# Where the third and fourth chunk of the attention output are split, and which buffers the last stretch splits into: a two-layer graph attention kernel

## The chip, the core and the metric

The kernel runs on one core of a Trainium2 chip. The metric is the device time of one execution in microseconds (us). TensorE (PE) does the matrix products and has a row of its own, PEld, for its weight loads. VectorE (DVE), ScalarE (ACT) and GpSimd (POOL) do the element work, and the queue of SyncE (SP) issues most of the remaining transfers.

## The reference

The input `x` is 64 matrices of 256 x 512 in fp32, `adj` is one 256 x 256 matrix of zeros and ones, and all five weights are 512 x 512.

```
# layer 0
q, k, v = x @ Wq + bq, x @ Wk + bk, x @ Wv + bv          # 8 heads of 64
scores  = q k^T / sqrt(64) + (1 - adj) * -1e9
o       = softmax(scores) v                                # per head, then side by side
x       = layernorm(x + o @ Wo + bo)
# layer 1
y       = adj @ x
x       = layernorm(x + y @ weight + bias)
```

## The kernel before

**Pairs and windows.** The 64 matrices are handled as 32 pairs (`NP` = 32), so that a product has 512 rows. The work is software-pipelined in windows: window `w` holds the attention of pair `w`, the v, q and k products of pair `w+1` ("ahead"), and the products with `Wo` (name "o") and with layer 1's weight (name "l") of pair `w-1` ("behind"). Windows 1 to 30 have one pattern, written out as a list of steps in `between` (L540); `last_window` (L598) finishes pairs 30 and 31, with a list of its own. The 29 windows from 2 to 30 have the same first half.

**Three parts.** An fp32 product is made of three passes in a faster matmul type. A left operand is split into three tiles by four instructions: on VectorE `cut` (the upper bits, L168), `low` (the rest, L169) and `diff` (L174), and on ScalarE `high`, a copy of `cut` (L298 or L278). The weights lie split in DRAM and are streamed in, three tiles of 1 MB for each product.

**Blocks.** One product of one of four row or column groups is a block (L532). `near` (L317) is eight matmuls, four with the low part and four with the high part, and then a ScalarE instruction that scales the PSUM bank (L326). `far` (L328) is the four matmuls with the diff part, and the evacuation: for "o" and "l" a VectorE addition onto the residual `r` (L338), in the last two pairs L342. `far` lags behind: `block` appends to `LAGGED`, and `caught_up(n)` (L524) works the list down to n entries. In a list of steps `f1` is `caught_up(1)` and `f0` or `f` is `caught_up(0)`. Four PSUM banks (`ps_mm`) serve all blocks, so the bank of a block must have been evacuated before the fourth block after it starts.

**Chunks.** `chunk_parts` (L284) splits one chunk of the attention output (`co[j]` or "o" chunk j below) or of adj @ x (`cl[j]`). Its tiles come from pools of their own: three buffers for high and low (`chunks`), four for diff (`differences`), and a single buffer for `cut`. The parts of x (`x_parts`, `x_diff`) come from another pool, `parts`, with four buffers each. What of x's four chunks does not fit in its window is kept in `PENDING` for the next one: from window 2 on its list is one chunk, `x_t` (a transpose, L264), `x_parts` and `x_diff`.

**Slots.** A slot is one quarter of a pair's attention: `values` of the unit before (sums with ones at L394, values at L402), then `scores` of its own (L367), exponentials on ScalarE (L371). `masked` (L374) multiplies each of the two tiles of exponentials with the mask on VectorE, `summed` (L380) adds the two. The next slot's first matmuls (L394) need that sum `sm`.

**Due times.** Such follow-up work is put off by `later(n, f)`, and falls due at the n-th `tick` after it. A tick follows every block, slot and `adj_x` step (L592), but not a `chunk_parts`, an x step or a `caught_up`. The first tick after a slot is its own, so `later(1, ...)` in a slot runs directly behind it.

**Whose order is written.** In windows 1 to 30 the orders of TensorE, ScalarE and VectorE are those of the list (`manual_schedule`, L639). In the last window only TensorE's order is written; the compiler's scheduler orders the others by readiness and by their place in the list.

Of the kernel before, what the change touches and what calls it, by code (L numbers as in the profile page):

```python
# [21 lines left out]
F32R = mybir.dt.float32r  # L22
# [5 lines left out]
P = 128  # L28
# [15 lines left out]
def fast(tc, x, adj, wq, bq, wk, bk, wv, bv, wo, bo, w1, b1, out):  # L44

    nc = tc.nc
    B, N, D = x.shape
# [3 lines left out]
    NP = B // 2  # L51
# [15 lines left out]
    parts = pool("parts", 4)  # L67
    chunks = pool("chunks", 3)
    differences = pool("differences", 4)
# [96 lines left out]
    def cut_low(a, cut, low):  # L166

        nc.vector.tensor_scalar(cut.bitcast(I32), a.bitcast(I32), -int(FINE), None, op0=OP.bitwise_and)  # L168
        nc.vector.tensor_tensor(low, a, cut, op=OP.subtract)  # L169

    def difference(a, low, diff):


        nc.vector.scalar_tensor_tensor(diff, low.bitcast(F32), -(FINE + 1), a, op0=OP.mult, op1=OP.add)  # L174
# [50 lines left out]
    def later(n, f, *args):  # L225
        due.append([n, f, args])
# [9 lines left out]
    BANKS = {}  # L236

    def x_t(p, i):  # L240
        xs = XC.pop((p, i))
        if p == 0:
            pt = ps_mm.tile([P, DC, P], F32, name="mm")
            if i == 0:
                for d in range(DC):
                    if d % 2 == 0:
                        t = qk.tile([P, 2, D], F32, name="kT")
                    XF[p, d] = t[:, d % 2]
            for d in range(DC):
                nc.tensor.transpose(pt[:, d, :], xs[:, d * P:(d + 1) * P], ident)  # L250
            for d in range(DC):
                to = XF[p, d][:, i * P:(i + 1) * P]
                if d % 2:
                    nc.scalar.activation(to, pt[:, d], AF.Copy)
                else:
                    nc.vector.tensor_copy(to, pt[:, d])
        else:
            if p > 1:
                XF[p, i] = xpool.tile([P, D], F32, name="xT")
                XC[p, i] = xs  # L260
            elif i % 2 == 0:
                t = four.tile([P, 2, D], F32, name="o")
                XF[p, i], XF[p, i + 1] = t[:, 0], t[:, 1]
            nc.vector.transpose(XF[p, i], xs)  # L264
            if p == 1:
                load_next()
# [17 lines left out]
    def chunk_parts(name, p, j):  # L284

        a = (O if name == "o" else Y)[p, j // 2][:, j % 2].rearrange("p k i -> p (k i)")
        cut = one.tile([P, D], F32, name="cut")
        high, low = (chunks.tile([P, D], F32R, name=n) for n in ("chigh", "clow"))
        diff = differences.tile([P, D], F32R, name="cdiff")
        cut_low(a, cut, low)  # L290
        difference(a, low, diff)
        CP[name, p, j] = high, low, diff
        CUT[name, p, j] = cut
        later(1, chunk_high, name, p, j)
# [64 lines left out]
    def scores(p, u):  # L359
        g, b = UNITS[u]  # L360
        for kc in range(NC):

            sc = [ps_at.tile([P, 2, N], F32, name="at") for s in range(2)]
            for a in range(2):
                for s in range(2):
                    r = slice(s * HD, (s + 1) * HD)
                    nc.tensor.matmul(sc[s][:, a, :], K[p, g][r, a, b, kc * P:(kc + 1) * P], Q[p, g][r, a, b, :],  # L367
                                     start=True, stop=True)
            e = E[p, u, kc] = one.tile([P, 2, 2, N], F32, name=f"e{kc}")
            for s in range(2):  # L370
                nc.scalar.activation(e[:, s], sc[s], AF.Exp, scale=qscale)  # L371
            later(1 + kc, masked, p, u, kc)

    def masked(p, u, kc):  # L374
        e = E[p, u, kc].rearrange("p s a n -> p (s a) n")
# [164 lines left out]
    def between(w):  # L540

        ahead, behind = w + 1, w - 1
        b = lambda name: [(block, name, behind if name in "ol" else ahead, j) for j in range(4)]
        v, q, k, o, l = (b(n) for n in "vqkol")
        c = lambda name, p: [(chunk_parts, name, p, j) for j in range(4)]
        y = [(adj_x, behind, i) for i in range(4)]
        bo_steps = [(with_bo, w, b) for b in range(2)]
        x_steps = [(x_t, w + 2, i) for i in range(4) if w + 2 < NP]
        x1 = [[s for f in (x_t, x_parts) for s in [(f, w + 2, i)] if w + 2 < NP] for i in range(4)]
        x2 = [[(x_diff, w + 2, i)] if w + 2 < NP else [] for i in range(4)]  # L550
        slot, f1 = [None], [(caught_up, 1)]
        f0 = [(caught_up,)]
        split = lambda name: [(split_w, name, i) for i in range(4)]
        mixed = lambda m, n: [s for pair in zip(m, n) for s in pair]
        halves_tiles = lambda: [one.tile([P, 2, D], F32, name=f"hl{i}") for i in range(2)]
        if w == -1:
            return [(x_t, 0, i) for i in range(4)] + mixed(v, split("v")) + mixed(q, split("q")) + [(adj_t,)] + \
                mixed(k, x_steps)
        if w == 0:
            raw_weight("o", halves_tiles(), nc.sync)  # L560
            PENDING[:] = [s for m, n in zip(x1, x2) for s in m + n]
            return slot + mixed(v, split("k")) + slot + q[:3] + split("o") + [(bv_wo,), (load_w, 3)] + \
                [(lambda: raw_weight("l", halves_tiles(), nc.sync),)] + slot + q[3:] + k[:2] + split("l") + \
                [(load_r, 0)] + slot + k[2:] + bo_steps + c("o", w)[:2] + \
                [(load_w, 3), (load_r, 1)]
        co, cl = c("o", behind), c("l", behind)
        seq = slot + co[2:3] + o[:1] + f1 + co[3:] + o[1:2] + PENDING[:6] + o[2:] + PENDING[6:] + slot + v + q[:1] + slot + q[1:] + f1 + \
            y[:1] + f0 + y[1:2] + k[:1] + (cl[:1] if w < NP - 2 else []) + y[2:] + f0 + bo_steps + slot + k[1:2] + \
            (cl[1:2] if w < NP - 2 else [])
        PENDING[:] = x1[3] + x2[3]  # L570
        if w == NP - 2:
            co = c("o", w)
            return seq + k[2:3] + co[:1] + k[3:] + co[1:2] + [(block, "o", w, 0)] + cl[:1] + [(block, "o", w, 1)] + cl[1:2]
        seq += k[2:3] + cl[2:3] + k[3:] + x1[0] + l[:1] + f1 + x2[0] + x1[1] + x2[1] + l[1:2] + cl[3:] + \
            l[2:3] + c("o", w)[:1] + x1[2] + x2[2] + l[3:] + f1 + c("o", w)[1:2]
        return seq

    PENDING = []
# [6 lines left out]
    def steps(seq, units):  # L585
        for step in seq:
            if step is None:
                before = units.pop(0)
                step = slot, before, units[0]
            f, *args = step  # L590
            f(*args)
            if f in (block, slot, adj_x, values, split_w):  # L592
                tick()
# [4 lines left out]
    def last_window():  # L598

        p, q = NP - 2, NP - 1  # L600
        for name, r in (("o", p), ("l", p - 1)):
            for i in range(3):
                for to in range(r + 1, NP):
                    WP[name, to, i] = WP[name, r, i]

        def rows_of_q():

            R[q] = [four.tile([P, NC, D], F32, name="v") for b in range(2)]
            for b in range(2):
                nc.sync.dma_start(R[q][b], xr[q][:, b])  # L610

        pairs = {"r": p - 1, "p": p, "q": q}

        def some(what):


            for word in what.split():
                if word == "slot":
                    yield None
                elif word == "f":  # L620
                    yield (caught_up,)
                elif word[0] == "y":
                    yield from ((caught_up,), *((adj_x, pairs[word[1]], 2 * int(word[2]) + i) for i in range(2)))
                else:
                    yield chunk_parts if word[0] == "c" else block, word[-3], pairs[word[-2]], int(word[-1])

        bo_steps = [(with_bo, q, b) for b in range(2)]
        seq = [None, (rows_of_q,), *some("lr0 cop2 lr1 cop3 op2 clr2 op3 clr3 f slot yp0 lr2 yp1"), *bo_steps,
               *some("slot coq0 lr3 coq1 oq0 clp0 oq1 clp1 f slot lp0 clp2 lp1 clp3 yq0"), (values, q, 3),
               *some("lp2 coq2 lp3 coq3 oq2 clq0 oq3 f clq1 lq0 lq1 yq1 clq2 clq3 lq2 lq3 f")]  # L630
        steps(seq, [(p, 3), (q, 0), (q, 2), (q, 1), (q, 3)])
        while due:
            tick()
# [8 lines left out]
    with tc.manual_schedule(engines={mybir.EngineType.PE}):  # L642
        last_window()
# [188 lines left out]
```

## Time and profile before

| | |
|---|---|
| median of 3 runs | 2554.0 us (2552.22 to 2556.43) |
| profiled execution | 2553.1 us, TensorE clock granted 0.995 |
| busy, PE / PEld / DVE / ACT / POOL | 98% / 74% / 73% / 67% / 15% |
| window (1143.80 to 1221.18 us) | 77.38 us |
| PE idle before matmuls, by waits: on `clow`, of DVE | 24.6 us in 33 waits |
| all other waits of PE's matmuls together | 22.9 us |

The page lists how long each engine was busy, slices the span, and names for each group of instructions the idle time of its engine just ahead of it and what ended that. A window's stretch of the trace shows the same matter instruction by instruction: start, duration, engine, line, output and inputs by their names. Wait times in the trace are the idle of the engine's data path; an instruction behind a wait may start a little later still than the end of the idle.

### The profile page before, as it was taken

To read this page: it belongs to the slowest core of one execution; us is meant where nothing else is said; L and a number is where in the kernel's file an instruction comes from. 1 tells how busy PE (TensorE), PEld (TensorE's weight loads), DVE (VectorE), ACT (ScalarE), POOL (GpSimd) and SP (SyncE) were. 2 spreads that over 40 slices of the span, in tenths; PEclk is the share of its full clock that TensorE was granted. 3 is DMA by queue.
4 is the path that set the end of the run, shared out by engine and by line. 5 is a ranking of instruction groups with operands and counts; after the bars stand their busy time and mean duration, and the time that the engine had idled before them with its cause. 6 is when DMAs were issued, how large, how long until landed. Compare 5 with 4: busy or idle time off the path is not lost.

```text
span 2553.1 us, 42184 instructions
## 1 busy us (share of the span) xinstructions
PE 2496.0 (98%) x15806; PEld 1886.6 (74%) x15806; DVE 1872.6 (73%) x3239; ACT 1705.7 (67%) x3206; POOL 382.4 (15%) x793
## 2 busy tenths in 40 slices
PE   8999999999999999999999999999999999999997
PEld 4477777777777777777777777777777777777765
DVE  4676787677886677876767876768876778866786
ACT  4557666776666766666776667766667766677755
POOL 0111111111111111111111111111111111111101
PEclk9999999999999999999999999999999999999998
DMA  7868778778788687777787787787787787777711
GB/s 205 284 201 273 235 232 259 240 244 243 240 256 247 236 263 232 235 250 252 231 274 226 232 259 243 240 262 234 246 246 247 251 247 233 247 254 229 257 68 51
DMA packets 375744, 600.25 MB, mean 235 GB/s; under 512 B 273520, under 2 KB 273776, under 8 KB 317552
## 3 DMA queue, kind: packets, MB, share of 16 engines
q0 software_dynamic: 65232, 475.03, 51.9%
q1 hardware_dynamic: 309760, 121.42, 22.0%
q8 instruction: 127, 2.08, 0.3%
q10 hardware_dynamic: 544, 1.05, 0.1%
q14 instruction: 81, 0.66, 0.1%
HBM read 548.15 MB, written 49.28 MB: 234 GB/s over the span
## 4 chain that ended last, share of the span: by engine, by line
PE 70%; DVE 25%; issue 3%; DMA 1%; ACT 0%; POOL 0%; SPq 0%; DVEq 0%; ACTq 0%
PE mm L314 50%; PE at L367 7%; PE at L402 6%; PE mm L512 5%; DVE clow L169 4%; DVE r L338 3%; DVE cdiff L174 3%; DVE diff L174 2%; DVE cut L168 2%; PE at L394 2%; DVE e L376 2%; DVE low L169 2%; DVE xT L264 2%; DVE x L168 1%; DVE o L418 1%
## 5 line engine op out<-in xcount | busy, mean ns | idle before, releaser
L326 ACT ACTIVATE mm<-mm 128x512 f32<-128x512 f32 x616 | 357.8, 581 | 356.7 <-PE mm L314 356.6
L376 DVE TENSOR_TENSOR e<-e,adjT 128x1024 f32<-128x1024 f32 x256 | 307.6, 1221 | 34.2 <-ACT e L371 34.2
L314 PE MATMUL mm<-wr,clow 128*128 128x512 f32 x1024 | 285.1, 401 | 25.1 <-DVE clow L169 24.6
L371 ACT ACTIVATE e<-at 128x512 f32<-128x512 f32 x512 | 265.2, 604 | 52.9 <-PE at L367 52.9
L314 PE MATMUL mm<-wr,chigh 128*128 128x512 f32 x1024 | 279.9, 396 | 0.7
L314 PE MATMUL mm<-wr,cdiff 128*128 128x512 f32 x1024 | 269.6, 391 | 5.9 <-ACT mm L326 5.9
L314 PE MATMUL mm<-low,wr 128*128 128x512 f32 x960 | 265.1, 398 | 0.0
L314 PE MATMUL mm<-high,wr 128*128 128x512 f32 x960 | 257.2, 390 | 0.0
L367 PE MATMUL at<-qT,kT 64*128 64x256 f32 x2048 | 256.6, 389 | 0.1
L314 PEld LDWEIGHTS mm<-wr,clow 128*128 128x128 f32 x1024 | 188.7, 190 | 86.6 <-DVE clow L169 38.3
L314 PE MATMUL mm<-diff,wr 128*128 128x512 f32 x960 | 248.5, 391 | 0.0
L402 PE MATMUL at<-e,v 128*32 128x256 f32 x4096 | 246.9, 381 | 0.0
L367 PEld LDWEIGHTS at<-qT,kT 64*128 64x128 f32 x2048 | 190.6, 186 | 67.7 <-issue 53.0
L499 DVE TENSOR_TENSOR hl<-r,hl 128x512 fp32r<-128x512 f32 x122 | 84.3, 691 | 203.4 <-ACT hl L498 203.4
L314 PEld LDWEIGHTS mm<-wr,chigh 128*128 128x128 f32 x1024 | 191.5, 189 | 53.0 <-ACT chigh L298 14.2
L314 PEld LDWEIGHTS mm<-wr,cdiff 128*128 128x128 f32 x1024 | 192.5, 188 | 48.1 <-ACT mm L326 7.8
L444 ACT ACTIVATE z<-r,mean 128x512 bf16<-128x512 f32 x240 | 172.6, 719 | 76.2 <-DVE mean L436 71.2
L314 PEld LDWEIGHTS mm<-low,wr 128*128 128x128 f32 x960 | 173.6, 188 | 51.6 <-issue 19.9
L338 DVE SCALAR_TENSOR_TENSOR r<-mm,r 128x512 f32<-128x512 f32 x240 | 160.4, 687 | 69.6 <-PE mm L314 69.6
L314 PEld LDWEIGHTS mm<-high,wr 128*128 128x128 f32 x960 | 180.3, 188 | 38.4
L476 ACT ACTIVATE r<-r,less,rstd 128x512 f32<-128x512 f32 x248 | 200.4, 808 | 6.1 <-DVE less L469 6.1
L314 PEld LDWEIGHTS mm<-diff,wr 128*128 128x128 f32 x960 | 176.3, 188 | 33.6
(123 smaller groups left out, 3985.0 us busy)
## 6 DMA issues: line engine op xcount, KB each, us to landing
wr<-o POOLq DMA_DIRECT2D x93, 1024.0 KB, 6.3
wr<-v POOLq DMA_DIRECT2D x90, 1024.0 KB, 6.4
wr<-q POOLq DMA_DIRECT2D x90, 1024.0 KB, 6.5
wr<-k POOLq DMA_DIRECT2D x90, 1024.0 KB, 7.3
wr<-l POOLq DMA_DIRECT2D x90, 1024.0 KB, 7.6
x<-in_x_dram SPq DMA_DIRECT2D x496, 64.0 KB, 6.4
r<-in_x_dram SPq DMA_DIRECT2D x31, 1024.0 KB, 5.3
out_dram<-r SPq DMA_DIRECT2D x60, 512.0 KB, 6.5
```

What stands on the lines that cost most here:

```text
L169: nc.vector.tensor_tensor(low, a, cut, op=OP.subtract)
L174: nc.vector.scalar_tensor_tensor(diff, low.bitcast(F32), -(FINE + 1), a, op0=OP.mult, op1=OP.add)
L314: nc.tensor.matmul(pm, *operands(name, p, j, i, k), start=k == 0 and i == begins, stop=k == DC - 1, skip_group_check=True)
L326: nc.scalar.activation(pm, pm, AF.Copy, scale=1 + 1 / FINE)
L338: nc.vector.scalar_tensor_tensor(r, pm, 1.0, r, op0=OP.mult, op1=OP.add, accum_out=ST[p, name][:, j:j + 1])
L367: nc.tensor.matmul(sc[s][:, a, :], K[p, g][r, a, b, kc * P:(kc + 1) * P], Q[p, g][r, a, b, :], start=True, stop=True)
L371: nc.scalar.activation(e[:, s], sc[s], AF.Exp, scale=qscale)
L376: nc.vector.tensor_tensor(e, e, mask[:, kc:kc + 1, :].to_broadcast([P, 4, N]), op=OP.mult)
L402: nc.tensor.matmul(at[h * 32:(h + 1) * 32, a, :], V[p, b][:, kc, col:col + 32], e[kc][:, h % 2, h // 2, :], start=kc == 0, stop=kc == NC - 1)
L444: nc.scalar.activation(waste, R[p][j // 2][:, j % 2], AF.Square, bias=mean[:, j:j + 1], accum_out=squares[:, j:j + 1])
L476: nc.scalar.activation(r, r, AF.Identity, scale=rstd, bias=less)
L512: nc.tensor.matmul(pm[:, j, :], hl[:, i, mc, j * P:(j + 1) * P], adjT[:, mc, :], start=mc == 0 and i == 0, stop=mc == NC - 1 and i == 1)
```

## The change

Four edits. In windows 2 to 30 the second mask of the first slot (`later` at L372) falls due one tick later. In all windows from 1 on, chunk 3 of the attention output is split directly behind the first "o" block, ahead of the `caught_up(1)` that used to come first. From window 2 on the pending chunk of x is split after the third "o" block and no longer after the second. And in the last stretch the nine chunks left in `DEEP` (of most products the second and the fourth) take their tiles from the pool of x's parts, and the list of the last window asks for chunks in pairs, up to four blocks ahead of their use. Its purpose is that TensorE should find each chunk's parts ready. The order of TensorE's blocks is not changed anywhere.

```diff
+    DEEP = [("l", NP - 3, 1), ("l", NP - 3, 3)] + [(n, p, j) for n in "ol" for p in (NP - 2, NP - 1) for j in (1, 3)]
+    DEEP.remove(("o", NP - 2, 1))
...
         cut = one.tile([P, D], F32, name="cut")
-        high, low = (chunks.tile([P, D], F32R, name=n) for n in ("chigh", "clow"))
-        diff = differences.tile([P, D], F32R, name="cdiff")
+        if (name, p, j) in DEEP:
+            high, low, diff = (parts.tile([P, D], F32R, name=n) for n in ("high", "low", "diff"))
+        else:
+            high, low = (chunks.tile([P, D], F32R, name=n) for n in ("chigh", "clow"))
+            diff = differences.tile([P, D], F32R, name="cdiff")
...
-            later(1 + kc, masked, p, u, kc)
+            later(1 + kc * (1 + (u == 0 and 1 < p < NP - 1)), masked, p, u, kc)
...
+        x_now = (PENDING[:6], [], PENDING[6:]) if w == 1 else ([], PENDING[:], [])
         co, cl = c("o", behind), c("l", behind)
-        seq = slot + co[2:3] + o[:1] + f1 + co[3:] + o[1:2] + PENDING[:6] + o[2:] + PENDING[6:] + slot + v + q[:1] + slot + q[1:] + f1 + \
+        seq = slot + co[2:3] + o[:1] + co[3:] + f1 + o[1:2] + x_now[0] + o[2:3] + x_now[1] + o[3:] + x_now[2] + slot + v + q[:1] + slot + q[1:] + f1 + \
...
-        seq = [None, (rows_of_q,), *some("lr0 cop2 lr1 cop3 op2 clr2 op3 clr3 f slot yp0 lr2 yp1"), *bo_steps,
-               *some("slot coq0 lr3 coq1 oq0 clp0 oq1 clp1 f slot lp0 clp2 lp1 clp3 yq0"), (values, q, 3),
-               *some("lp2 coq2 lp3 coq3 oq2 clq0 oq3 f clq1 lq0 lq1 yq1 clq2 clq3 lq2 lq3 f")]
+        seq = [None, (rows_of_q,), *some("cop2 cop3 lr0 clr2 lr1 clr3 op2 op3 f slot yp0 lr2 yp1"), *bo_steps,
+               *some("slot coq0 coq1 lr3 clp0 clp1 oq0 oq1 f clp2 clp3 slot lp0 lp1 yq0"), (values, q, 3),
+               *some("coq2 coq3 lp2 lp3 clq0 clq1 oq2 oq3 f lq0 lq1 yq1 clq2 clq3 lq2 lq3 f")]
```

In the last list r, p and q are pairs 29, 30 and 31; `lr0` is a block, `cop2` splits a chunk (c, name o, pair p, chunk 2), `yp0` is half of adj @ x.

## The prediction

> **What bounds the kernel now.** I read the page's busy times first, then its group with the largest TensorE idle, then one window, TensorE and VectorE side by side.
>
> ```profile
> PE 2496.0 (98%) x15806; PEld 1886.6 (74%) x15806; DVE 1872.6 (73%) x3239; ACT 1705.7 (67%) x3206; POOL 382.4 (15%) x793
> L314 PE MATMUL mm<-wr,clow 128*128 128x512 f32 x1024 | 285.1, 401 | 25.1 <-DVE clow L169 24.6
> ```
>
> TensorE sets the time; of its idle, half stands ahead of matmuls that read `clow`. The list of waits, stretch by stretch, shows 29 of these 33 at an even spacing of 77.4 us (215.3 to 2381.8 us), each 0.60 or 0.61 us: one in each window from 2 to 30. There is no other TensorE wait in these windows. In the timeline of one of them, TensorE:
>
> ```profile
> 1213.03 1.20 PE L314 MATMUL mm<-wr,clow 128*128 128x512 f32 x4
> ...
> 1217.69 1.07 PE L314 MATMUL mm<-wr,clow 128*128 128x512 f32 x4
> 1218.60 1.07 PE L314 MATMUL mm<-wr,chigh 128*128 128x512 f32 x4
> 1219.50 1.07 PE L314 MATMUL mm<-wr,cdiff 128*128 128x512 f32 x4
> 1221.18 1.21 PE L314 MATMUL mm<-wr,clow 128*128 128x512 f32 x4 [0.60 <-DVE clow L169]
> 1222.40 1.20 PE L314 MATMUL mm<-wr,chigh 128*128 128x512 f32 x4
> 1223.44 1.08 PE L314 MATMUL mm<-wr,cdiff 128*128 128x512 f32 x4
> 1224.45 0.64 PE L394 MATMUL at<-sm,ones 128*32 128x256 f32 x8
> ```
>
> These are block o0 (1213.03), o2 (1217.69), the far half of o0, the block o3 that waits, the far half of o1, and the next slot. Undisturbed, groups start 0.91 us apart (1217.69, 1218.60, 1219.50), and a slot 1.0 us after the last group. From 1219.50 the slot is thus due at 1219.50 + 3 x 0.91 + 1.0 = 1223.2; it starts at 1224.45. The wait costs 1.23 us, twice the 0.60 shown: both the restart and the chigh group behind it come late. VectorE in the same stretch:
>
> ```profile
> 1215.11 1.22 DVE L376 TENSOR_TENSOR e<-e,adjT 128x1024 f32<-128x1024 f32 x1
> 1216.25 0.42 DVE L168 TENSOR_SCALAR cut<-o 128x512 int32<-128x512 int32 x1
> 1218.04 1.22 DVE L376 TENSOR_TENSOR e<-e,adjT 128x1024 f32<-128x1024 f32 x1
> 1219.17 0.68 DVE L338 SCALAR_TENSOR_TENSOR r<-mm,r 128x512 f32<-128x512 f32 x1
> 1219.98 0.42 DVE L168 TENSOR_SCALAR cut<-o 128x512 int32<-128x512 int32 x1
> 1220.43 0.69 DVE L169 TENSOR_TENSOR clow<-o,cut 128x512 fp32r<-128x512 f32 x1
> 1221.77 1.22 DVE L382 TENSOR_TENSOR sm<-e,e 128x1024 f32<-128x1024 f32 x1
> ```
>
> First mask, chunk 2, second mask, residual of l3, chunk 3, sum. VectorE runs without a gap from 1205.3 to 1228.7; the clow of chunk 3 ends at 1221.12, and TensorE starts 0.06 us later. So here VectorE's order decides, although it is 73% busy on average.
>
> The last stretch is another case:
>
> ```profile
> 2443.80:2506.40 62.60, 53.27 (x367) 39.67 (x366) 58.99 (x125) 40.22 (x74) 7.27 (x15) 0.98 0.12 43
> 2504.57 1.86 PE L512 MATMUL mm<-adjT,hl 128*128 128x256 f32 x7 [3.01 <-DVE hl L499]
> 2507.22 3.64 PE L402 MATMUL at<-e,v 128*32 128x256 f32 x32
> ```
>
> The first line is a table by stretch: length, then PE, PEld, DVE, ACT. Here DVE is busy 59.0 of 62.6 us. TensorE's waits from 2443 us on add up to 14.5 us; only 0.66 and 2.17 of them are on `clow`, 5.9 are on the scaling by ScalarE and 3.0 on `hl`. After the 3.0 us the 32 value matmuls took 3.64 us, where elsewhere they take 1.91.
>
> **What the Trainium skill says.** "TensorE: Matmul & The Clock Gate", Part 1, has the array fall to half its clock after an idle window of about 3.4 us; the 3.64 against 1.91 us after 3.01 us of idle agrees in kind. The same page's specifications call VectorE's and ScalarE's queues strict FIFO: the trace agrees, the clow of chunk 3 stands behind a mask and a residual that nobody waits for yet. "Perfetto Trace Analysis", Optimization Strategy, says that consistent bubbles can mean too few buffers for the next tile. In the windows the bubble recurs 29 times, but VectorE is busy then, not waiting for a buffer: order, not room.
>
> **The change in the windows.** No instruction is added or removed. I lay out VectorE's new order from the same start, with steps from start to start in the lines above: mask 1.14, chunk 1.79 (1216.25 to 1218.04), second mask 1.13, residual with its mean 0.81 (1219.17 to 1219.98), plain residual 0.61 (1225.44 to 1226.05), sum 1.22 to its end.
>
> - First mask at 1215.11, chunk 2 at 1216.25: unchanged.
> - Chunk 3 now follows at 1218.04; its clow ends at 1218.04 + 0.45 + 0.69 = 1219.2. TensorE wants it at 1219.50 + 0.91 = 1220.41: **1.2 us to spare**. Its single `cut` is free: ScalarE's chigh of chunk 2 ended at 1217.33. Its diff buffer is that of l3, read by TensorE until 1216.04.
> - Residual of l3 at 1219.83, evacuated at 1219.83 + 0.68 = 1220.51. It now lies behind chunk 3, and block o3 takes just this bank (four banks: l3, o0, o1, o2). Block o3 starts at about 1220.57, some 0.16 late, and the slot could begin at 1220.57 + 1.03 + 0.91 + 1.0 = 1223.51 (1.03: a first group after a stop).
> - Second mask, one tick later, at 1220.64; residual of o0 at 1221.77; sum from 1222.38 to 1223.60. Before, it ended at 1222.99 with 1.46 us to spare. The slot's first matmul needs it, so it starts at about **1223.66**: a new wait of about 0.15 us.
> - The pending x chunk goes behind the sum, 1223.5 to 1226.0, ahead of the residual of o1. Its low part ends at about 1225.4; the v block needs it as fourth matmul, at about 1228.6. Nothing lost. ScalarE's copy for it ends at about 1225.4 and holds back the next slot's zc by less than 0.5 us; the attention bank that zc reads is wanted later than that, by the second half of the scores.
> - On ScalarE chigh of chunk 3 goes ahead of the squares, which wait for the mean 0.66 us longer than before; that hides behind TensorE's work, since the scaling of o2 is needed only in the v blocks.
>
> So the slot moves from 1224.45 to 1223.66, 0.79 us; I take off 0.04 for the restart and use **0.75 us a window**. The later work of VectorE ends at the same instant as before, 0.75 nearer to TensorE, but from 1229.0 it idles again (1.47, 0.88, 4.00 us in the next 12 us), so nothing piles up. 29 x 0.75 = **21.8 us**. Bounds: 0.3 a window if the two waits restart badly, 1.23 if neither shows.
>
> Window 1 doesn't change: `LAGGED` is empty there and its other edits are switched off.
>
> **The change in the last stretch.** Chunks no longer queue for three buffers: four more sets stand open, those of x, whose last readers are the k blocks of window 30. But VectorE's work up to 2506 us is the same, and it has only 62.6 - 59.0 = 3.6 us of idle to give. Chunks asked for earlier can only take the place of residuals, statistics and `hl`, on which the largest waits hang. I expect the 0.66 and part of the scaling waits to go, and take 2.5 us. Bounds: all of the 9.3 us of waits up to 2506 less what VectorE can't give, 3.6, and the half clock behind the 3.0 us wait (3.64 - 1.91, and 0.4 in the sums ahead of it, 2.1), together -6; and +4 if two chunks (2 x 1.79) get ahead of `hl`. The end, 9 us from the last matmul on, is the same.
>
> Sum: 2554.0 - 21.8 - 2.5 = 2529.7, **2530 us**.
>
> **Rivals.**
> 1. *The wait is gone altogether* (neither the bank nor the sum is late): 2554 - 29 x 1.23 - 2.5 = 2516. Against it: the sum's place behind 8.5 us of gapless VectorE work.
> 2. *The wait mostly moves*: bank and sum cost two restarts like the one now, whose cost was twice its idle; 0.3 us a window: 2554 - 8.7 - 2.5 = 2543. For it: the present 0.60 cost 1.23. Against it: that came from a late chigh, which now is early.
> 3. *The last stretch gets worse*, `hl` behind the chunks, +8, the windows as forecast: 2554 - 21.8 + 8 = 2540.
> 4. *Slower*: the sum comes so late that the windows give nothing, and the last stretch loses 6 more: 2560.
>
> **Chances.** Forecast 0.62, rival 1 0.12, rival 2 0.14, rival 3 0.08, rival 4 0.04. The range of 2518 to 2542 leaves out the rivals 1 and 4 and part of rival 2. Faster by over 0.2% (under 2549): all but rival 4 and a little of rival 2, 0.95; within: 0.02; slower: 0.03.
>
> **What would show it.** Windows of 76.6 us instead of 77.37. No wait on `clow` in windows 2 to 30; in its place a short one on `sm` ahead of L394, perhaps one on `r` (L338) ahead of block o3. On VectorE the order mask, cut, cut, residual, mask, residual, sum, xT. In the last stretch pairs of cuts close together and the 3.0 us wait on `hl` not longer. Wrong if a window keeps 77.3, if the wait on `sm` is over 0.5 us, or if the stretch from 2443 us changes by more than 6.

## The result, and the profile after

| kernel | median, us | against before |
|---|---|---|
| before | 2555.2 (4 runs) | |
| changed | 2536.6 (4 runs, 2533.95 to 2538.65) | 0.9928, 95% interval 0.9911 to 0.9946 |
| forecast | 2530 (2518 to 2542) | |

The kernel is 18.6 us faster; the forecast was 24. The page of the changed kernel, busy times and the group that led the idle before:

```profile
PE 2492.1 (98%) x15806; PEld 1895.2 (75%) x15806; DVE 1870.3 (74%) x3239; ACT 1709.9 (67%) x3206; POOL 386.1 (15%) x793
...
L321 PE MATMUL mm<-wr,clow 128*128 128x512 f32 x988 | 273.5, 399 | 9.7 <-DVE clow L169 5.6
```

Nobody has less to do (VectorE 1870 us against 1873), and the idle on `clow` is down from 24.6 to 5.6 us. (The lines are shifted: L314 is now L321, L394 L402, L376 L384, L338 L345, L382 L390. 36 matmuls, four for each of nine chunks, are gone from this group because the deep chunks' tiles are named `low`.) TensorE in one window of the changed kernel; its 1214.28 answers to 1217.69 of before:

```profile
1214.28 1.07 PE L321 MATMUL mm<-wr,clow 128*128 128x512 f32 x4
1215.19 1.07 PE L321 MATMUL mm<-wr,chigh 128*128 128x512 f32 x4
1216.10 1.07 PE L321 MATMUL mm<-wr,cdiff 128*128 128x512 f32 x4
1217.31 1.20 PE L321 MATMUL mm<-wr,clow 128*128 128x512 f32 x4
1218.34 1.07 PE L321 MATMUL mm<-wr,chigh 128*128 128x512 f32 x4
1219.25 1.07 PE L321 MATMUL mm<-wr,cdiff 128*128 128x512 f32 x4
1220.47 0.64 PE L402 MATMUL at<-sm,ones 128*32 128x256 f32 x8 [0.15 <-DVE sm L390]
```

No wait on `clow` is left, but the rhythm of 0.91 us is still broken three times: 1.21 to block o3 (0.30 too long), 1.03 behind its first group (0.12), and 1.22 to the slot instead of 1.00 (0.22). These 0.64 us are left of the 1.23. From slot to slot a window is 76.79 to 76.88 us, 76.82 on average, where it was 77.38. VectorE in the same stretch:

```profile
1211.71 1.22 DVE L384 TENSOR_TENSOR e<-e,adjT 128x1024 f32<-128x1024 f32 x1
1212.84 0.42 DVE L168 TENSOR_SCALAR cut<-o 128x512 int32<-128x512 int32 x1
...
1214.63 0.42 DVE L168 TENSOR_SCALAR cut<-o 128x512 int32<-128x512 int32 x1
1215.16 0.69 DVE L169 TENSOR_TENSOR clow<-o,cut 128x512 fp32r<-128x512 f32 x1
1215.95 0.69 DVE L174 SCALAR_TENSOR_TENSOR cdiff<-clow,o 128x512 fp32r<-128x512 f32 x1
1216.56 0.68 DVE L345 SCALAR_TENSOR_TENSOR r<-mm,r 128x512 f32<-128x512 f32 x1
...
1217.37 1.22 DVE L384 TENSOR_TENSOR e<-e,adjT 128x1024 f32<-128x1024 f32 x1
1218.50 0.68 DVE L345 SCALAR_TENSOR_TENSOR r<-mm,r 128x512 f32<-128x512 f32 x1
...
1219.11 1.22 DVE L390 TENSOR_TENSOR sm<-e,e 128x1024 f32<-128x1024 f32 x1
```

That is the forecast order: mask, cut, cut, residual, mask, residual, sum. The clow of chunk 3 ends at 1215.85, 1.2 us before TensorE asks for it at 1217.01. The residual of l3 ends at 1217.24, and block o3, which takes its bank, starts 0.07 us later. The sum ends at 1220.33, and the slot starts 0.14 us later.

**Where the 18.6 us come from.** The trace splits at the second slots of windows 2 and 30. The 28 windows between them took 2385.03 - 218.58 = 2166.45 us before and 2372.84 - 221.84 = 2151.00 after: 15.45 us less, and with window 2's own about 16. From window 30's slot to the end it was 2553.1 - 2385.03 = 168.1 us and is 2536.9 - 2372.84 = 164.1: 4.0 less. The part up to window 2's slot was 3.3 us longer, although up to the start of window 2 TensorE, VectorE and ScalarE have the same instructions in the same order. That part differs by 4 to 5 us between the kernels here, but it repeats where a kernel was profiled twice: up to window 2's first slot it took 206.8 and 206.6 us in the changed kernel (e11 below), 202.5 and 202.7 in that of e4, and 202.9 before. So it seems to go with the kernel as built, and why isn't known. Single times of one kernel scatter by up to 6 us. The length of a window repeats within 0.1 us, its average within 0.03, and is the better measure.

In the last stretch of the changed kernel, TensorE around the wait on `hl`:

```profile
2489.34 1.20 PE L520 MATMUL mm<-adjT,hl 128*128 128x256 f32 x8 [1.31 <-DVE hl L507]
...
2493.84 2.15 PE L410 MATMUL at<-e,v 128*32 128x256 f32 x32
```

The wait of 3.01 us is now 1.31 (and one of 0.66 on statistics behind it); one on a residual grew from 0.51 to 1.65. All waits of this stretch together went from 14.5 to 11.9 us. The 32 value matmuls take 2.15 us instead of 3.64, but that isn't the change's doing, as e1 shows.

### The profile page after: what moved, and what is told of

It reads as the page before. It is cut to its first block, busy times and chain, and to the rows that moved or that the text cites. A ratio compares the mean times of both kernels' runs of the same rounds, so it can differ in the third digit from the quotient of the medians.

```text
span 2536.9 us, 42179 instructions
## 1 busy us (share of the span) xinstructions
PE 2492.1 (98%) x15806; PEld 1895.2 (75%) x15806; DVE 1870.3 (74%) x3239; ACT 1709.9 (67%) x3206; POOL 386.1 (15%) x793
## 4 chain that ended last, share of the span: by engine, by line
PE 68%; DVE 25%; issue 3%; DMA 1%; ACT 1%; POOL 0%; SPq 0%; DVEq 0%; ACTq 0%
PE mm L321 48%; PE at L374 7%; PE at L410 6%; PE mm L520 5%; DVE clow L169 4%; DVE cdiff L174 3%; DVE r L345 3%; DVE diff L174 3%; DVE cut L168 2%; PE at L402 2%; DVE low L169 2%; DVE xT L268 2%; DVE e L384 1%; DVE sm L390 1%; DVE x L168 1%
## 5 line engine op out<-in xcount | busy, mean ns | idle before, releaser
L384 DVE TENSOR_TENSOR e<-e,adjT 128x1024 f32<-128x1024 f32 x256 | 307.2, 1220 | 26.5 <-ACT e L378 26.5
L321 PE MATMUL mm<-wr,clow 128*128 128x512 f32 x988 | 273.5, 399 | 9.7 <-DVE clow L169 5.6
L321 PE MATMUL mm<-wr,chigh 128*128 128x512 f32 x988 | 266.0, 391 | 0.0
L321 PE MATMUL mm<-low,wr 128*128 128x512 f32 x960 | 264.9, 398 | 0.0
L321 PE MATMUL mm<-wr,cdiff 128*128 128x512 f32 x988 | 260.6, 390 | 3.8 <-ACT mm L333 3.8
L321 PE MATMUL mm<-high,wr 128*128 128x512 f32 x960 | 257.1, 390 | 0.0
L321 PE MATMUL mm<-diff,wr 128*128 128x512 f32 x960 | 248.4, 390 | 0.0
L321 PEld LDWEIGHTS mm<-wr,clow 128*128 128x128 f32 x988 | 180.7, 188 | 68.7 <-DVE r L345 16.4
L321 PEld LDWEIGHTS mm<-wr,cdiff 128*128 128x128 f32 x988 | 185.9, 188 | 43.7 <-ACT mm L333 4.6
L321 PEld LDWEIGHTS mm<-wr,chigh 128*128 128x128 f32 x988 | 186.2, 189 | 40.5 <-ACT chigh L305 0.8
L321 PEld LDWEIGHTS mm<-low,wr 128*128 128x128 f32 x960 | 173.5, 188 | 51.8 <-issue 19.9
L321 PEld LDWEIGHTS mm<-high,wr 128*128 128x128 f32 x960 | 180.2, 188 | 38.5
L345 DVE SCALAR_TENSOR_TENSOR r<-mm,r 128x512 f32<-128x512 f32 x240 | 162.5, 686 | 60.5 <-PE mm L321 60.5
L321 PEld LDWEIGHTS mm<-diff,wr 128*128 128x128 f32 x960 | 176.2, 188 | 33.7
```

The source lines that it names most:

```text
L321: nc.tensor.matmul(pm, *operands(name, p, j, i, k), start=k == 0 and i == begins, stop=k == DC - 1, skip_group_check=True)
L345: nc.vector.scalar_tensor_tensor(r, pm, 1.0, r, op0=OP.mult, op1=OP.add, accum_out=ST[p, name][:, j:j + 1])
L384: nc.vector.tensor_tensor(e, e, mask[:, kc:kc + 1, :].to_broadcast([P, 4, N]), op=OP.mult)
```

## The experiments

**e1 and e2: the two halves alone.** e1 has the edits of the windows with the last stretch of before, e2 the other way round:

```diff
 # e1, against the changed kernel: DEEP = [], and the old three lines of the last list
 # e2, against the changed kernel:
-            later(1 + kc * (1 + (u == 0 and 1 < p < NP - 1)), masked, p, u, kc)
+            later(1 + kc, masked, p, u, kc)
-        x_now = (PENDING[:6], [], PENDING[6:]) if w == 1 else ([], PENDING[:], [])
+        x_now = (PENDING[:6], [], PENDING[6:])
-        seq = slot + co[2:3] + o[:1] + co[3:] + f1 + o[1:2] + ...
+        seq = slot + co[2:3] + o[:1] + f1 + co[3:] + o[1:2] + ...
```

> The three edits of the windows alone; the last stretch has its old list and its old buffers. Theory (the gain is an order on VectorE in the windows, and the last stretch gives a few us of its own): windows of 76.80 us as in the changed kernel, against 77.37 before, so 29 x 0.57 = 16.5 us faster than before, about 2538; the stretch from the last slot of window 30 to the end as long as before. Rival (what the windows save is partly handed back in the last stretch, or the other way round): 3 us or more away from 2538 with the same window.

> The last stretch alone: new list, nine chunks in the buffers of x's parts; the windows as before. Theory: windows of 77.37 us, the stretch behind window 30 about 3.4 us shorter than before, 2552 in all. Rival (the last stretch gains nothing, its 3.4 us were an effect of an earlier start): within 1 us of before.

e1: 2540.9 us against 2555.9, ratio 0.9945 (0.9928 to 0.9961), so 15.1 us; windows of 76.80 to 76.86. e2: 2550.7, ratio 0.9983 (0.9975 to 0.999), so 5.3 us; windows of 77.38, and 164.15 us from window 30's slot to the end. The halves add up: 15.1 + 5.3 = 20.4 against 18.6 measured for both, inside the scatter (by the ratios, 14.1 and 4.3 against 18.4). The last stretch gains by itself, so the rival of a mere knock-on from the earlier start falls. In e1, where the wait on `hl` is still 3.01 us, the value matmuls behind it take 2.27 us; in the second profile of the changed kernel (e11) they take 2.76:

```profile
2493.68 2.27 PE L410 MATMUL at<-e,v 128*32 128x256 f32 x32
2492.87 2.76 PE L410 MATMUL at<-e,v 128*32 128x256 f32 x32
```

So their time doesn't follow the wait, and about 1.5 of the 4.0 us that the last stretch gained in the trace (3.64 to 2.15) can't be credited to the change.

**e3: chunk 3 where it was.** Of the windows' edits only the second mask and the chunk of x stay moved.

```diff
-        seq = slot + co[2:3] + o[:1] + co[3:] + f1 + o[1:2] + ...
+        seq = slot + co[2:3] + o[:1] + f1 + co[3:] + o[1:2] + ...
```

> The changed kernel, but chunk 3 is split where it was, behind the residual of l3; only the second mask and the chunk of x stay moved (and the last stretch). Theory (the second mask, not chunk 3's place, made chunk 3 late; behind the mask's move the bank of l3 and the sum decide): clow of chunk 3 ends 0.4 us before it is needed, no wait on the bank of l3, the sum up to 0.14 earlier[...]; windows of 76.66 to 76.80 us, 0 to 4 us faster than the changed kernel. Rival (chunk 3 directly behind chunk 2 is what brings the gain): a wait on clow again, windows of 77.2 or more, 2548 or more.

2530.1 us, ratio 0.9901 (0.9885 to 0.9918): 6.5 us faster than the changed kernel in its first timing. Windows are 76.66 to 76.72. TensorE at block o3 and the slot:

```profile
1212.47 1.07 PE L321 MATMUL mm<-wr,cdiff 128*128 128x512 f32 x4
1213.37 1.07 PE L321 MATMUL mm<-wr,clow 128*128 128x512 f32 x4
...
1215.26 1.07 PE L321 MATMUL mm<-wr,cdiff 128*128 128x512 f32 x4
1216.70 0.64 PE L402 MATMUL at<-sm,ones 128*32 128x256 f32 x8 [0.37 <-DVE sm L390]
```

Block o3 is on time (0.90 us behind the group ahead of it), and what remains is the wait for the sum alone, longer than in the changed kernel because TensorE is earlier. So the mask's later due time is what brought chunk 3 in time; moving chunk 3 as well cost the change some 0.14 us a window, 4 us in all. It is the sum that sets the slot in both kernels: counted from the start of the first mask it ends 8.49 us later here and 8.62 in the changed kernel, and the slot moves by the same 0.13. The bank that came late there cost nothing beyond that.

The rest of the 6.5 us lies in the start (205.0 us up to window 2's first slot, against 206.8) and in the end: 161.4 us from window 30's slot, against 164.1 and 162.65 in the two profiles of the changed kernel. The list of the end is the same, and so are its waits up to that on `hl` (1.30 us) and that on statistics (0.66). From there to the next block the granted clock was 0.74 and 0.75 in the changed kernel's two profiles, and 1.00 here:

```profile
2486.59 1.91 PE L410 MATMUL at<-e,v 128*32 128x256 f32 x32
```

So the end differs by the clock that was granted, not by the order; why it falls in one execution and not in another stays open.

**e4 and e10: the sum ahead of the residual of o0.** What was left stands behind that residual, so e4 makes the sum directly behind the second mask:

```diff
 # against e3
-            later(1, summed, p, u)
+            summed(p, u) if u == 0 and 1 < p < NP - 1 else later(1, summed, p, u)
```

> As e3_chunk3_back, and the sum of the first slot directly behind its second mask, ahead of the residual of o0 (0.61 us). Theory (what was left of the wait stood behind this residual and the bank): sum 0.6 us earlier, no TensorE wait in the window but perhaps a short one on chigh; windows of 76.14 to 76.25 us, 2517 to 2521 in all. Rival (VectorE's gapless work in this stretch pins the window, and the wait only moves on, to x's parts or to the next bank): windows of 76.6 to 76.8, 2532 to 2537.

2515.7 us, ratio 0.9846 (0.9829 to 0.9862). Windows of 76.20 to 76.26 us and no TensorE wait listed in any of them:

```profile
1204.08 1.07 PE L321 MATMUL mm<-wr,cdiff 128*128 128x512 f32 x4
1204.98 1.07 PE L321 MATMUL mm<-wr,clow 128*128 128x512 f32 x4
1205.89 1.13 PE L321 MATMUL mm<-wr,chigh 128*128 128x512 f32 x4
1206.86 1.07 PE L321 MATMUL mm<-wr,cdiff 128*128 128x512 f32 x4
1207.86 0.64 PE L402 MATMUL at<-sm,ones 128*32 128x256 f32 x8
```

From the first of these groups to the slot it is 3.78 us; it was 4.95 before, 4.37 in the changed kernel, and 3.72 without any wait. VectorE has the same instructions as ever here; only their order differs. It was timed once more, beside the changed kernel on one chip (e11):

> The kernel of e4_sum_first once more, beside the changed kernel on the same chip: 2514 to 2518 us, 18 to 22 less than the changed kernel.

> The changed kernel once more: 2534 to 2538 us; windows of 76.80 us, and a start (up to window 2) that differs from the first profile by up to 4 us with the same instructions.

2518.0 us (0.9859, 0.9844 to 0.9874) for e10 and 2535.1 (0.9926, 0.9912 to 0.9939) for the changed kernel. **It beats both kernels**, the changed one by 17 us here.

**e5 and e6: single edits on the kernel before.** Chunk 3's place alone, and the second mask alone:

```diff
 # e5, against before
-        seq = slot + co[2:3] + o[:1] + f1 + co[3:] + o[1:2] + ...
+        seq = slot + co[2:3] + o[:1] + co[3:] + f1 + o[1:2] + ...
 # e6, against before
-            later(1 + kc, masked, p, u, kc)
+            later(1 + kc * (1 + (u == 0 and 1 < p < NP - 1)), masked, p, u, kc)
```

> Of the change only chunk 3's place: split directly behind block o0, ahead of the residual of l3; second mask, chunk of x and last stretch as before. Theory (the residual of l3 frees the bank that block o3 takes, and with the second mask still ahead it comes too late): no wait on clow, but block o3 waits for the residual, over 1 us; windows of 77.6 to 77.9 us, slower than before by 7 to 15 us. Rival (chunk 3's place is the gain): windows of 76.8 or less.

> Of the change only the second mask's later due time; chunk 3, the chunk of x and the last stretch as before. Theory (without x's move the sum stands behind x's chunk and the residual of o0 on VectorE): clow of chunk 3 in time, the slot waits for the sum, which ends about 1226.1 where the timeline of before has the slot at 1224.45; windows of 78.5 to 79.2 us, 35 to 53 us slower than before. Rival (x's chunk doesn't matter for the sum): windows of 76.7.

e5: 2565.2 us in one run against 2553.9, windows of 77.70 to 77.76 (one of 78.08). From its list of TensorE's waits (total, times, longest):

```profile
PE mm L321 <- DVE r L345: 37.3, 29, 1.6
```

The wait on `clow` has left the windows, and block o3 waits for the residual of l3 instead, 1.27 us in most windows: the bank. e6: 2628.2 us in one run, 74 slower. One of its windows:

```profile
1258.65 0.64 PE L402 MATMUL at<-sm,ones 128*32 128x256 f32 x8 [2.90 <-DVE sm L390]
1259.08 2.98 PE L410 MATMUL at<-e,v 128*32 128x256 f32 x32
```

With x's chunk still ahead of it, the sum comes 2.9 us late. The 79.2 us of the expectation was right for 16 of the 28 windows between the second slots of windows 2 and 30; 11 others take 80.8, because I hadn't counted what follows such an idle: here the value matmuls run at 2.98 us instead of 1.91, with a granted clock of 0.81 from the idle to the end of the scores. So each of these two edits alone is a loss, and it is the mask with x's chunk that gains. No run moved x's chunk alone; in the kernel before it stands behind both chunk 3 and the sum, so by the order it can't hold them up there.

**e7 and e8: list or buffers.** The last stretch's list with all chunks in their old pools (e7: `DEEP = []` on top of e2), and the nine chunks in x's buffers with the old list (e8).

```diff
 # e7, against e2
-    DEEP.remove(("o", NP - 2, 1))
+    DEEP = []
 # e8, against e2: the last list
-        seq = [None, (rows_of_q,), *some("cop2 cop3 lr0 clr2 lr1 clr3 op2 op3 f slot yp0 lr2 yp1"), *bo_steps,
+        seq = [None, (rows_of_q,), *some("lr0 cop2 lr1 cop3 op2 clr2 op3 clr3 f slot yp0 lr2 yp1"), *bo_steps,
...
```

> Of the change only the new list of the last stretch, all chunks in their old pools of three and four buffers. Theory (list and buffers belong together: chunks asked for early have to wait for one of three buffers): less than half of the 5.3 us that both bring, 2553 to 2556. Rival (the place in the list alone decides, three buffers are enough): 2550 to 2551.

> Of the change only the buffers: nine chunks in the tiles of x's parts, with the old list of the last stretch. Theory (buffers without requests ahead bring little): within 2 us of before, 2554 to 2556. Rival (the old list was held up by the three buffers, and they alone bring the gain): 2550 to 2551.

2552.6 and 2552.9 us against 2553.9, both 0.9995 (0.9986 to 1.0004): neither can be told from no change, while both together gave 5.3 us. But these totals hide the last stretch. From window 30's slot to the end it takes 165.6 us with the list alone and 166.5 with the buffers alone, against 168.1 before and 164.15 with both, and the starts of these two kernels are 2.4 and 1.4 us longer than before. In the traces the list alone brings the wait on `hl` down to 1.3 us and leaves 5.7 on ScalarE's scaling; the buffers alone leave 3.0 on `hl` and 5.0 on the scaling; together it is 1.3 and 4.7. The waits on `clow` and `low` add up to 2.5 us with the list alone and to 2.5 with both. One profile of the last stretch is good to 1.4 us at best (the changed kernel's two). So whether list and buffers need each other or simply add up (2.5 and 1.6 against 3.9) isn't shown.

**e9: chunk 3 moved, sum first.** e4's sum in the changed kernel, with chunk 3 directly behind chunk 2.

> As e4_sum_first, but with chunk 3 directly behind chunk 2 as in the change, so that the residual of l3 stands behind it. Theory (chunk 3's place costs the bank of block o3: 0.30 us late, 0.12 in the restart): windows of 76.5 to 76.6 us against 76.2. Rival (the bank never mattered, the sum was the whole remainder): 76.2.

2530.1 us in one run; windows of 76.57 to 76.64, as the theory has it. TensorE:

```profile
1211.60 1.07 PE L321 MATMUL mm<-wr,cdiff 128*128 128x512 f32 x4
1212.81 1.21 PE L321 MATMUL mm<-wr,clow 128*128 128x512 f32 x4
...
1215.80 0.64 PE L402 MATMUL at<-sm,ones 128*32 128x256 f32 x8
```

The step to block o3 is again 1.21 us, the slot comes without a wait. In this window the list shows no idle for the 0.30 us, as in the changed kernel: found only by comparing starts. Against e4, chunk 3's place costs about 0.37 us a window, over 10 us.

## Why the prediction was right, and where it was off

**The sign and the place.** The gain is in the 29 windows, by an order on VectorE, and the wait on `clow` is gone; e1 shows 15 of the 18.6 us there. The cost of that wait, 1.23 us for an idle of 0.60, is borne out by e4, which has recovered nearly all of it (77.38 - 76.22 = 1.16). A part of it was ScalarE's order. Before, block o3's chigh group starts 1.22 us behind its clow group, 0.31 too long, directly behind this copy, whose `cut` had ended at 1220.40 while ScalarE was busy with squares:

```profile
1221.73 0.62 ACT L298 ACTIVATE chigh<-cut 128x512 fp32r<-128x512 f32 x1
```

In the changed kernel the copy runs ahead of the squares, as forecast.

**The mis-sized term: 0.75 us a window, measured 0.57.** 29 x 0.18 = 5 us, of the 5.4 by which the forecast missed. The profiles show two more misses, of opposite sign: the start took 3.8 us longer, which the prediction had at nothing, and the last stretch gave 1.5 more than forecast. That the total came as near as it did is in part luck. The working named both waits that would be left, the bank behind the residual of l3 and the sum behind the residual of o0, and had them too short: 0.16 and 0.15 us, with 0.12 for a restart between them, where 0.30, 0.22 and 0.12 were lost. Its step for a chunk, 1.79 us, was taken from chunk 2. Chunk 3 in its new place takes 0.53 us from cut to clow and 0.79 to cdiff; all other chunks of the windows, and chunk 3 back in its old place (e3, e4), take 0.45 and 0.73. So the residual, the second mask and the sum all come 0.14 us later than the forecast has them. And the sum reached TensorE 0.14 us after its end, where I had taken the 0.06 seen behind clow. Together that is 0.22, and 0.79 - 0.22 is the 0.57 that was measured. Why two instructions take longer in this one place no trace shows.

**What I credited wrongly.** The prediction took the change as one, with chunk 3's new place at its centre ("1.2 us to spare"). That spare time was true and worth nothing: e3 and e4 against e9 show that chunk 3 in the old place is in time once the second mask is out of its way, and that moving it put the bank's evacuation behind it. The prediction saw that bank, and didn't ask what the other order would give.

**"The later work of VectorE ends at the same instant", and x's parts lose nothing:** right, to the same 0.14 us. No wait for x's parts or for a later bank appears in windows 2 to 30, not even in e4, where TensorE is another 0.6 us earlier.

**The last stretch: 2.5 us predicted, 4.0 in the trace, 5.3 in e2.** The wait of 0.66 us that was to go is still there, now on `low`, the same chunk in another buffer. The scaling waits went from 5.9 to 4.7, as expected. Of what I had only as a bound, the wait on `hl` shrank by 1.7 us; that the slow matmuls behind it went from 3.64 to 2.15 us is the chance shown at e1. The waits alone fell by 2.6 us, close to the forecast. "TensorE: Matmul & The Clock Gate", Part 1, fits these runs in kind, not in size: it has the clock halve after an idle window of about 3.4 us, and here shorter idles were enough, 2.9 us in 13 of 29 windows of e6, and 1.31 and 0.66 us close together in the changed kernel (granted clock 0.74). That such idles left the clock alone in the other 16 windows, and in e3, fits the page's window, which runs free of the kernel; how it counts wasn't tested.

**The rivals.** Rival 1, no wait left, 2516, was the wrong account of this change and is nearly the time of e4. Rival 2, most of the wait moved on, has part of the truth: about half of the 1.23 us, 0.64, did move. On "Perfetto Trace Analysis", Optimization Strategy, by which such repeated bubbles can mean too little room for the next tile, I wrote order, not room. That held for the wait that was removed, and for what took its place: e3 frees the bank in time, and the slot comes earlier only by as much as the sum does. Room, a PSUM bank not yet evacuated, decides where the sum doesn't: 1.27 us of idle in e5, 0.37 us a window in e9.

**Still open:** why the start is up to 4 us longer in some kernels, the changed one among them, and when the clock falls behind a short idle.

## What to carry to other kernels

When a wait repeats once in each period, write out the blocked engine's order up to the next thing the bound engine needs, with a deadline for each item, and sort by deadlines: here residual of l3 (bank), chunk 3, second mask and sum, and only then the residual of o0 and x's chunk. An instruction brought forward delays everything it overtakes, and one of those may free the very bank that its own consumer needs. And compare the same stretch of two traces before an edit is given up: with e7 a start that was 2.4 us longer hid the 2.5 us that the last stretch gained in its trace.

## What was not expected of the hardware

- An idle of 0.60 us of the data path cost 1.23 us, 0.31 of it by a ScalarE copy that came late as well, and elsewhere 0.30 us were lost with no idle listed: starts, not waits, show the loss.
- From start to start two VectorE steps took 0.07 us more in one place of the order than in all others (0.53 for 0.45, 0.79 for 0.73); the cause is open.
- The same idle of 2.9 us is followed by slow matmuls in some windows and not in others; in e6 that makes windows of 79.2 and of 80.8 us. In the last stretch the clock fell to 0.74 behind two waits of 2.0 us together, and in e3 not at all.
